# An adaptive-norm block with attention and routed experts: GpSimd's order bound by edges, experts' numbers read earlier, tile fills moved behind the first norm

## The chip, the cores and the metric

One Trainium2 chip, one of its cores. A core has TensorE (PE, with its weight loads PEld), VectorE (DVE), ScalarE (ACT), GpSimd (POOL) and SyncE (SP), each with an instruction stream of its own, and DMA queues that are issued from SP, ACT and POOL. The metric is the device time of one execution in microseconds (us), lower is better.

## The reference

A transformer block over x of 4 x 512 x 256, all in float32: a modulated layer norm, causal attention with 32 heads of 8 (8 key heads), a gated residual, a second modulated norm, then 16 routed experts (4 of them per token, chosen within 2 of 4 groups) plus a shared expert, and a second gated residual.

```python
mod = (_silu(L0_c) @ L0_wmod).reshape(L0_c.shape[0], 6, 1, -1)
sa, ca, ga, sb, cb, gb = (mod[:, 0], mod[:, 1], mod[:, 2], mod[:, 3], mod[:, 4], mod[:, 5])
ga = (2 * (ga >= 0) - 1) * jnp.maximum(jnp.abs(ga), 0.25)
gb = (2 * (gb >= 0) - 1) * jnp.maximum(jnp.abs(gb), 0.25)
h = _layernorm(x, axis=-1) * (1 + ca) + sa
x = x + ga * _L0_attn_ref(h, L0_attn_wq, L0_attn_wk, L0_attn_wv, L0_attn_wo)
h = _layernorm(x, axis=-1) * (1 + cb) + sb
x = x + gb * _L0_ffn_ref(h, ...)

# _L0_attn_ref: q, k, v projections, softmax(q k^T / sqrt(8), causal) v, projection wo
# _L0_ffn_ref:
cw = _combine_weights(xt, gate_w)          # softmax, 2 of 4 groups, top 4, normalized
out = jnp.zeros_like(xt)
for e in range(E):
    a = _swiglu(xt @ expert_up_w[e].T)
    out = out + cw[:, e:e + 1] * (a @ expert_down_w[e].T)
out = out + _swiglu(xt @ shared_up_w.T) @ shared_down_w.T
```

## The kernel before

**A plan makes the order.** The kernel does not write its instructions down in sequence. Each step is added to a `Plan` with its engine, an estimated cost, what it needs, a due time and the buffers that it takes and gives. `plan.go` takes, again and again, the step that can start first by these estimates (the earlier due time breaks a tie) and only then emits its instructions. The block runs under a manual schedule for PE, DVE, ACT and SP: on these four the emitted order is the order on the chip. POOL is not in that list; there a scheduler of the framework orders the instructions itself, whatever order the plan had for them. Each engine runs its stream in order; an instruction that waits holds all behind it.

**Start.** SP loads x for the first batch, then c, the modulation weights and the projections' weights (L178, L482 to L487). DVE fills three pairs of key and query tiles, `kx` with -1 and `qx` with 0 (L489, L490); POOL makes constants and fills two `vaug` tiles with 0 and, for the softmax denominators, a 1 beside each head's values (L492, L495). `norm1` of batch 0 follows: `stats` on DVE (L585, L586), `root` (L590), `power` on POOL (L594), `normalize` on DVE (L599), transposes on PE (L643), the modulation on ACT (L650), for which `modulate_first` (L519) and `modulated` (L528, L529) prepare the factors. `split` projects queries and keys (L695), cuts them into three bf16 parts (L705 to L718) and stores them to DRAM (L723); `project_v` and `place` (L750, L761) put the values into `vaug`. `load(s)` brings the parts of one pack of heads into `qx[s % 3]` and `kx[s % 3]` (L778 on SP, L783 on ACT for the first two packs, on SP later). After that SP issues the later loads (x of the other batches, gate, shared and output weights) and `blank_all`, which clears the two accumulators `acc_d` in DRAM.

**Attention** runs over 16 packs s, four for each batch. `row_max` multiplies queries by keys (L821), masks (L829) and takes row maxima on DVE (L842); `shift` turns the maxima into three rows of `qx` (L881, L891, L901). `pack` multiplies again with the maxima in place (L962), ACT takes the exponential (L974, tile `ex`, five buffers), POOL zeroes what lies above the diagonal (L980, 12 selects a pack), and `weigh` multiplies by `vaug` on PE (L932). After a batch's fourth pack, `after` projects by `wo` (L1081) and gates on DVE (L1091, tile `ao`), POOL adds to x (L1099), and `norm2` normalizes again: POOL's `power` (L594) and `modulate` (L1126, L1127, four times two instructions), the router's logits and choice on DVE, and then 16 indirect DMAs from POOL (L1297), each of which scatters 128 token rows from `row` (one buffer) to the lists of their experts in `rows_d`. Batches 0 to 2 do this while later packs run; batch 3 after attention.

**Experts.** `make_table` on DVE finds for each of 79 blocks of 128 rows its expert (`of_i`) and its first row (`row_i`). The shared expert's steps (L394 to L448) run on PE among and before the first blocks. A block j goes: `fetch` on SP (seven buffers of x), `turn` on PE (transposes, tile pt, L1454), `copy` on ACT (xt, L1458), `meta` on DVE (token and weight, L1463, L1466), `up` on PE (pu, L1474), `silu` on ACT (L1484), `product` on DVE (a_b, L1488), `turn_back` on PE (pb, L1493), `copy_back` on DVE (at_b, L1497), `down` on PE (py, L1502), `weigh` on ACT (y_b, L1512), and `put` on POOL: an indirect DMA that adds 128 rows into `acc_d[j % 2]` (L1515). `up` and `down` read the weights at an address that depends on the expert: `read` (L367) loads the block's number from SBUF into a register of PE's sequencer, at the beginning of `up`:

```python
def up():
    st["e"] = read(t["of_i"], j, PE, E - 1)
    st["pu"] = psu.tile([P, 2 * I], F32, name="pu")
```

In the order that the plan made, a steady period on PE is pu(42), py(41), pt(44), pb(42), then the load of number 43 and pu(43). At the end the two accumulators are read back, summed, gated and added to x (L1567 to L1578).

Of the kernel before, what the change touches and what calls it, by code (L numbers as in the profile page):

```python
# [151 lines left out]
def kernel(  # L152
# [122 lines left out]

    def hold(name, bufs=1):
        return rooms.setdefault(name, Room(bufs)).hold()
# [97 lines left out]
    def shared(b, due, up_bank, down_bank, first=None):  # L375
# [3 lines left out]
        def unit(n):  # L379
# [45 lines left out]
            for i in range(half // P):  # L425
# [20 lines left out]
                def put(i=i):  # L446
                    xs = x_sb[:, b * NT + n * half // P + i, :]
                    nc.gpsimd.tensor_tensor(xs, xs, st["o", i], ALU.add)  # L448
# [7 lines left out]
                plan.add("POOL", 0.75, put, [ga], due(), gives=[o_hold])  # L456
# [9 lines left out]
    def attention():  # L466
        with ExitStack() as ectx:
# [20 lines left out]
            for n, (q, k) in enumerate(zip(qx, kx)):  # L488
                nc.vector.memset(k, -1.0)  # L489
                nc.vector.memset(q, 0.0)  # L490
            for t in vaugs:
                nc.gpsimd.memset(t, 0.0)  # L492
                for g in range(NG):
                    one = VW * (g % SLOTS) + HD
                    nc.gpsimd.memset(t[:, :, g, one : one + 1], 1.0)  # L495
# [8 lines left out]
            plan.free.update(PE=6.0, ACT=4.0, DVE=5.0, POOL=8.0, SP=4.0)  # L504
# [71 lines left out]
            def layernorm(b, needs, due):  # L576
# [15 lines left out]
                def power():  # L592
                    st["rs"] = work.tile([P, NT], F32, name="rs")
                    nc.gpsimd.tensor_tensor(st["rs"], st["ve"], mhalf, ALU.pow)  # L594
# [20 lines left out]
                op = plan.add("POOL", 1.05, power, [op], due())  # L615
# [16 lines left out]
            def norm1(b, due):  # L632

                first = [later, weighed.get(NPK * (b - 1) - 1)] if b else []
                st, ops, h = layernorm(b, [first, [], [], []], due)
                ht_hold = hold("ht")
# [105 lines left out]
            def project_v(b, last, due, ht_hold):  # L742
# [24 lines left out]
                valued[b] = plan.add("ACT", 0.6, place, [op], due(), gives=[p_hold])  # L767
# [3 lines left out]
            def load(s):  # L771

                loaded[s] = []
                needs = [stored[True, s], stored[False, s], scored.get(s - 3)]
# [175 lines left out]
            def scores(s, j, c, r, n, exs, last, due):  # L950
# [27 lines left out]
                def select():  # L978

                    nc.gpsimd.affine_select(  # L980
                        out=st["ex"][:, :, 0:P],
                        in_=st["ex"][:, :, 0:P],
                        pattern=[[0, n], [1, P]],
                        base=0,
                        channel_multiplier=-1,
                        compare_op=ALU.is_ge,
                        fill=0.0,
                    )
# [6 lines left out]
                return pe, plan.add("POOL", 0.18 + 0.115 * n, select, [op], due), ex_hold  # L995
# [46 lines left out]
            def after(b, due):  # L1042
# [31 lines left out]
                for half in range(NT // 2):  # L1074
# [22 lines left out]
                    def put(half=half):  # L1097
                        xs = x_sb[:, b * NT + 2 * half : b * NT + 2 * half + 2, :]
                        nc.gpsimd.tensor_tensor(xs, xs, st["ao", half], ALU.add)  # L1099
# [9 lines left out]
                    adds.append(plan.add("POOL", 1.27, put, [ga], due(), gives=[ao_hold]))  # L1109
# [4 lines left out]
            def norm2(b, adds, due):  # L1114
# [5 lines left out]
                for i in range(NT):  # L1120

                    def modulate(i=i):
                        if i == 0:
                            st["row"] = work.tile([P, NT, XW], F32, name="row", bufs=1)
                        h = st["row"][:, i, 0:D]
                        nc.gpsimd.tensor_tensor(h, ln["xn"][:, i, :], m2_sb[:, b, 1, :], ALU.mult)  # L1126
                        nc.gpsimd.tensor_tensor(h, h, m2_sb[:, b, 0, :], ALU.add)  # L1127

                    rows.append(
                        plan.add(  # L1130
                            "POOL", 1.5, modulate, [ops[i], gates_made, *rows[-1:]], due(),
                            takes=[row_hold] if i == 0 else [],
                            gives=[ln_hold] if i == NT - 1 else [],
                        )
                    )
# [160 lines left out]
                def scatter(i, k):  # L1296
# [9 lines left out]
                    writes.append(dma.ins)  # L1306

# [19 lines left out]
                for i in range(NT):  # L1327
                    for k in range(TOPK):
                        final = i == NT - 1 and k == TOPK - 1
                        op = plan.add(  # L1330
                            "POOL", 1.3, lambda i=i, k=k: scatter(i, k), [op], due(),
                            lag=4.0 if final else 0.0 if b == B - 1 else 1.5, gives=[row_hold] if final else [],
                        )
# [24 lines left out]
            norm1(0, Pace(-8.0, -4.0, 40))  # L1358
            load(0)
# [24 lines left out]
    def ffn():  # L1384
# [48 lines left out]
        def block(j):  # L1433
# [17 lines left out]
            def turn():  # L1451
                st["pt"] = pst.tile([P, KC, P], F32, name="pt2")
                for k in range(KC):
                    nc.tensor.transpose(st["pt"][:, k, :], st["x"][:, ts(k, P)], ident)  # L1454

# [14 lines left out]
            def up():  # L1470
                st["e"] = read(t["of_i"], j, PE, E - 1)
# [52 lines left out]
            needs = [made, fetched[-1] if fetched else None]  # L1524
            if j == 0:
                needs += [*blanked, routed[B - 1]["rows"]]
            fe = plan.add("SP", 0.9, fetch, needs, due - 8, takes=[h["x"]])
            fetched.append(fe)
            op = plan.add("PE", 0.38, turn, [fe], due - 1.5, takes=[h["pt2"]])
# [5 lines left out]
                "PE", 1.45, up, [xt, weights], due, takes=[h["pu"]], gives=[h["xt"]]  # L1535
# [5 lines left out]
            op = plan.add("PE", 0.3, turn_back, [op], due + 0.6, takes=[h["pb"]], gives=[h["a_b"]])  # L1541
# [3 lines left out]
            op = plan.add("PE", 1.03, down, [op], due + 1.1, takes=[h["py"]], gives=[h["at_b"]])  # L1545
# [7 lines left out]
        fetched = []  # L1553
# [85 lines left out]
```

## Time and profile before

| | |
|---|---|
| median of three runs | 812.01 us (811.62 to 815.63) |
| the profiled execution | 819.83 us, its span 817.9 us |
| granted TensorE clock, mean over the span | 0.942 |
| start and first projections | 0 to 35 us |
| attention, 16 packs | 34 to 462 us |
| shared expert, routing of batch 3 | 462 to 560 us |
| expert blocks alone | 560 to 785 us |
| read-back and output | 785 to 818 us |
| PE busy, 150 to 200 / 200 to 250 / 250 to 300 us | 48.63 / 39.13 / 48.73 us |
| POOL: selects L980, 192 | 93.2 us busy, 491 ns each |
| POOL: scatters L1297, 64 | 63.9 us busy, 998 ns each |
| POOL: accumulating scatters L1515, 79 | 123.3 us busy, 1561 ns each |
| number loads on PE's sequencer, 79 | 295 / 507 / 585 ns (min / median / max) |

Times in a timeline are counted from the span's start. A line of the timeline has start, length, engine, line of the code, operation, output and input tiles, count, and in brackets the idle time of that engine just before, with what ended it. Matmuls are pipelined and their ends are modelled, so that PE's starts are safer to compare than its ends. Releasers are inferred from semaphores; where the engine named had long been done, it was another. The times below are worked out from the profiled execution.

### The profile page before, as it was taken

What the parts mean: (1) busy time and instruction counts of PE and PEld (TensorE: products, weight loads), DVE (VectorE), ACT (ScalarE), POOL (GpSimd) and SP (SyncE); (2) the same over time, 40 slices, a digit from 0 to 9 for tenths busy, and PEclk for the clock granted to TensorE, in tenths of its full rate; (3) what the DMA queues carried; (4) which work ended last, traced back from release to release, by engine and by line L of the source; (5) the groups of instructions that cost most, each with busy time, mean ns of one, the idle gap of its engine ahead of it and who ended that gap; (6) DMA issues with size and microseconds to landing.
All of it is one profiled execution on the core that took longest, in us unless ns stands there. A gap on an engine that the chain in (4) does not pass through costs nothing.

```text
span 817.9 us, 12877 instructions
## 1 busy us (share of the span) xinstructions
PE 686.4 (84%) x4205; PEld 417.4 (51%) x4236; DVE 454.4 (56%) x1286; ACT 309.9 (38%) x557; POOL 346.2 (42%) x449
## 2 busy tenths in 40 slices
PE   4568999999779998699968794999999999999930
PEld 3344455454434544245523483787666666666620
DVE  5395877878658887387854058343333333333318
ACT  1105655655345545264534510123333333333310
POOL 3001222344652355533555254514555555555533
PEclk9787999999999999899989997899999999999975
DMA  3484220202312023111111196604655655555465
GB/s 122 114 283 146 52 57 21 54 19 53 112 67 58 9 67 106 62 39 37 39 50 64 42 283 213 155 16 66 100 92 93 97 93 94 93 92 92 51 156 185
DMA packets 54969, 74.51 MB, mean 91 GB/s; under 512 B 8024, under 2 KB 48056, under 8 KB 53752
## 3 DMA queue, kind: packets, MB, share of 16 engines
q1 hardware_dynamic: 37992, 51.99, 22.8%
q0 software_dynamic: 14448, 19.31, 14.7%
q10 hardware_dynamic: 2464, 2.39, 0.9%
q8 instruction: 35, 0.57, 0.3%
q14 instruction: 30, 0.25, 0.1%
HBM read 41.11 MB, written 32.16 MB: 90 GB/s over the span
## 4 chain that ended last, share of the span: by engine, by line
PE 62%; DVE 19%; ACT 6%; issue 5%; POOL 4%; DMA 3%; another core or an unknown queue 1%; ACTq 0%; DVEq 0%; POOLq 0%
PE pu L1474 14%; PE py L1502 8%; PE pa L932 8%; PE pr L821 7%; DVE mx_s L842 6%; PE p L962 5%; PE pu L394 4%; ACT y_b L1512 4%; PE pr L829 3%; PE py L432 3%; PE p L543 2%; POOL rows_d L1297 2%; ACT ex L974 1%; PE p L695 1%; DMA s<-acc_d 1%
## 5 line engine op out<-in xcount | busy, mean ns | idle before, releaser
L842 DVE TENSOR_REDUCE mx_s<-pr 128x1 f32<-128x384 f32 (+3 forms) x352 | 213.2, 635 | 92.1 <-PE pr L829 67.4
L974 ACT ACTIVATE ex<-p 128x1024 f32<-128x1024 f32 (+1 forms) x192 | 163.5, 880 | 134.0 <-PE p L962 90.3
L980 POOL TENSOR_SCALAR_AFFINE_SELECT ex<-ex 128x256 f32<-128x256 f32 (+1 forms) x192 | 93.2, 491 | 206.9 <-ACT ex L974 205.1
L1515 POOL DMA_INDIRECT acc_d<-y_b,token x79 | 123.3, 1561 | 108.4 <-ACT xt L1458 97.7
L821 PE MATMUL pr<-kx,qx 125*128 125x384 bf16 (+3 forms) x512 | 127.2, 313 | 28.9 <-DVE mx_s L842 15.8
L1474 PE MATMUL pu<-up_sb,xt 128*128 x316 | 113.6, 482 | 12.7 <-ACT y_b L1512 11.4
L932 PE MATMUL pa<-ex,vaug 128*32 128x512 f32 (+3 forms) x1024 | 104.9, 452 | 20.0 <-POOL ex L980 10.5
L962 PE MATMUL p<-qx,kx 128*128 128x384 bf16 (+3 forms) x481 | 92.6, 300 | 6.0 <-DMA qx<-mrow 3.0
L1488 DVE TENSOR_TENSOR a_b<-sg_b,pu 128x176 f32<-128x176 f32 x79 | 26.7, 338 | 118.1 <-ACT sg_b L1484 118.1
L829 PE MATMUL pr<-seen,ident_h 128*128 128x128 bf16 (+2 forms) x352 | 89.5, 254 | 0.0
L821 PEld LDWEIGHTS <-qx 125*128 125x128 bf16 x512 | 47.4, 102 | 79.5 <-issue 51.8
L1502 PE MATMUL py<-down_sb,at_b 88*128 x316 | 81.4, 379 | 1.1 <-DVE at_b L1497 1.1
L1474 PEld LDWEIGHTS pu<-up_sb,xt 128*128 128x128 f32 x316 | 53.6, 189 | 47.7 <-ACT y_b L1512 26.6
L1297 POOL DMA_INDIRECT rows_d<-row,slot x64 | 63.9, 998 | 29.4 <-issue 16.2
L1502 PEld LDWEIGHTS py<-down_sb,at_b 88*128 88x128 f32 x316 | 59.7, 189 | 21.8 <-ACT y_b L1512 0.8
L1484 ACT ACTIVATE sg_b<-pu 128x176 f32<-128x176 f32 x79 | 25.1, 317 | 101.0 <-PE pu L1474 89.2
L962 PEld LDWEIGHTS <-kx 128*128 128x128 bf16 x512 | 41.2, 99 | 37.9 <-issue 23.1
L1512 ACT ACTIVATE y_b<-py,cw_b 128x256 f32<-128x256 f32 x79 | 37.4, 473 | 46.3 <-PE py L1502 46.3
L1497 DVE COPY at_b<-pb 88x256 f32<-88x256 f32 x79 | 33.2, 421 | 36.5 <-PE pb L1493 34.9
L932 PEld LDWEIGHTS pa<-ex,vaug 128*32 128x32 f32 x1024 | 22.3, 108 | 60.9 <-issue 34.0
L829 PEld LDWEIGHTS <-ident_h 128*128 128x128 bf16 x352 | 35.2, 100 | 31.0 <-issue 24.6
L394 PE MATMUL pu<-h2t,sup_sb 128*128 128x256 f32 (+1 forms) x192 | 47.8, 399 | 2.3 <-DVE a L414 1.7
(176 smaller groups left out, 760.1 us busy)
## 6 DMA issues: line engine op xcount, KB each, us to landing
x<-rows_d SPq DMA_DIRECT2D x79, 136.5 KB
qx<-qd SPq DMA_DIRECT2D x48, 192.0 KB
up_sb<-in_up_t SPq DMA_DIRECT2D x8, 704.0 KB
acc_d<-blank SPq DMA_DIRECT2D x2, 2176.0 KB
qd<-pt SPq DMA_DIRECT2D x16, 192.0 KB
down_sb<-in_down_t SPq DMA_DIRECT2D x8, 352.0 KB
rows_d<-blank SPq DMA_DIRECT2D x17, 136.5 KB
x_sb<-in_x SPq DMA_DIRECT2D x4, 512.0 KB
```

Source lines behind the costliest of these rows:

```text
L394: nc.tensor.matmul(st["p"][:rows, w, :], lhsT=sup_sb[:, k, c0 : c0 + rows], rhs=h2t[:, k, c1 : c1 + half], start=(k == 0), stop=(k == KC - 1),
L821: nc.tensor.matmul(pr[:, h, :], lhsT=qx[s % 3][:QKZ, REP * j + r + h, ts(i, P)], rhs=kx[s % 3][:QKZ, j, :w], start=True, stop=False, skip_ ...
L829: nc.tensor.matmul(pr[:, :, w - P :], lhsT=ident_h, rhs=seen.unsqueeze(1).to_broadcast([P, n, P]), start=False, stop=True, skip_group_chec ...
L842: nc.vector.tensor_reduce(mx[s][:, i, c0 : c0 + n], st["pr"], AX.X, ALU.max)
L932: nc.tensor.matmul(st["pa"][32 * r : 32 * r + 32, c * P :], lhsT=vaugs[b % 2][:, c, SLOTS * n + j, :], rhs=exs[r], start=(j == 0 and c == ...
L962: nc.tensor.matmul(pe[:, h, :], lhsT=kx[s % 3][:, j, ts(c, P)], rhs=qx[s % 3][:, REP * j + r + h, c * P :], start=True, stop=True,)
L974: nc.scalar.activation(ex, st["pe"], AF.Exp, scale=qk_scale)
L980: nc.gpsimd.affine_select(out=st["ex"][:, :, 0:P], in_=st["ex"][:, :, 0:P], pattern=[[0, n], [1, P]], base=0, channel_multiplier=-1, compa ...
L1297: dma = nc.gpsimd.indirect_dma_start(out=rows_d, out_offset=bass.IndirectOffsetOnAxis(ap=st["slot"][:, i, k : k + 1], axis=0), in_=st["row ...
L1474: nc.tensor.matmul(st["pu"], lhsT=st["xt"][:, k, :], rhs=up_sb[:, bass.ds(st["e"], 1), k, :].rearrange("p e f -> p (e f)"), start=(k == 0) ...
L1502: nc.tensor.matmul(st["py"], lhsT=st["at"][:, c, :], rhs=down_sb[:, bass.ds(st["e"], 1), c, :].rearrange("p e d -> p (e d)"), start=(c == ...
L1515: nc.gpsimd.indirect_dma_start(out=acc_d[j % 2], out_offset=bass.IndirectOffsetOnAxis(ap=st["token"][:, 0:1], axis=0), in_=st["y"], in_off ...
```

## The change

Three things. First, every POOL step of the plan is wrapped in `on_pool`, which adds an order-only dependency (no wait on the chip) from the instruction of POOL before it in the plan's order; scatters (`writes=True`) are ordered against what is not a scatter, but not among each other. Second, `read` moves from `up` to the end of `turn`, the planned costs of the block's PE steps change, and the planned chain from fetch to fetch is dropped. Third, the fills of `kx`, `qx` and `vaug` become steps of the plan: pair 0 and both `vaug` behind the last normalization of batch 0, pairs 1 and 2 behind the first query store; `load` and `place` now need them. The planned start times of the engines change a little.

```diff
+    stretches = [(False, []), (False, [])]
+
+    def on_pool(f, writes=False):
+        def run():
+            ins = [i.ins for i in f()]
+            if stretches[1][0] != writes:
+                stretches[:] = [stretches[1], (writes, [])]
+            (_, before), (_, same) = stretches
+            if not writes:
+                earlier = same[-1:] or before
+            else:
+                earlier = before[-1:]
+            nosync = mybir.DependencyInfo(
+                mybir.DependencyClass.NoSync, mybir.DependencyReason.DATA
+            )
+            for i in earlier:
+                tc.add_manual_dep(ins[0], i.name, nosync, reason="order on POOL")
+            same += ins
+
+        return run
...
-            for n, (q, k) in enumerate(zip(qx, kx)):
-                nc.vector.memset(k, -1.0)
-                nc.vector.memset(q, 0.0)
-            for t in vaugs:
-                nc.gpsimd.memset(t, 0.0)
+
+            def unused(n):
+                nc.vector.memset(kx[n], -1.0)
+                nc.vector.memset(qx[n], 0.0)
+
+            def denominators(t):
+                ins = [nc.gpsimd.memset(t, 0.0)]
                 for g in range(NG):
                     one = VW * (g % SLOTS) + HD
-                    nc.gpsimd.memset(t[:, :, g, one : one + 1], 1.0)
+                    ins.append(nc.gpsimd.memset(t[:, :, g, one : one + 1], 1.0))
+                return ins
+
+            filled, summed = [], []
+
+            def fill(after_it):
+
+                filled.append(plan.add("DVE", 2.7, lambda: unused(0), [after_it], -6.5))
+                for n, t in enumerate(vaugs):
+                    summed.append(
+                        plan.add(
+                            "POOL", 3.6, on_pool(lambda t=t: denominators(t)), [after_it], n - 6.5
+                        )
+                    )
...
-            plan.free.update(PE=6.0, ACT=4.0, DVE=5.0, POOL=8.0, SP=4.0)
+            plan.free.update(PE=6.5, ACT=5.0, DVE=5.0, POOL=6.0, SP=4.0)
...
-                op = plan.add("POOL", 1.05, power, [op], due())
+                op = plan.add("POOL", 1.05, on_pool(power), [op], due())
...
+                if b == 0:
+                    fill(ops[-1])
...
-                valued[b] = plan.add("ACT", 0.6, place, [op], due(), gives=[p_hold])
+                valued[b] = plan.add("ACT", 0.6, place, [op, summed[b % 2]], due(), gives=[p_hold])
...
-                needs = [stored[True, s], stored[False, s], scored.get(s - 3)]
+                needs = [stored[True, s], stored[False, s], scored.get(s - 3), filled[s % 3]]
...
-                return pe, plan.add("POOL", 0.18 + 0.115 * n, select, [op], due), ex_hold
+                return pe, plan.add("POOL", 0.18 + 0.115 * n, on_pool(select), [op], due), ex_hold
...
-                            "POOL", 1.3, lambda i=i, k=k: scatter(i, k), [op], due(),
+                            "POOL", 1.3, on_pool(lambda i=i, k=k: scatter(i, k), True), [op], due(),
...
             norm1(0, Pace(-8.0, -4.0, 40))
+            filled += [
+                plan.add("DVE", 2.7, lambda n=n: unused(n), [stored[False, 0]], -3.0)
+                for n in (1, 2)
+            ]
...
                 for k in range(KC):
                     nc.tensor.transpose(st["pt"][:, k, :], st["x"][:, ts(k, P)], ident)
+                st["e"] = read(t["of_i"], j, PE, E - 1)
...
             def up():
-                st["e"] = read(t["of_i"], j, PE, E - 1)
                 st["pu"] = psu.tile([P, 2 * I], F32, name="pu")
...
-            needs = [made, fetched[-1] if fetched else None]
-            if j == 0:
-                needs += [*blanked, routed[B - 1]["rows"]]
+            needs = [made, *blanked, routed[B - 1]["rows"]]
             fe = plan.add("SP", 0.9, fetch, needs, due - 8, takes=[h["x"]])
-            fetched.append(fe)
-            op = plan.add("PE", 0.38, turn, [fe], due - 1.5, takes=[h["pt2"]])
+            op = plan.add("PE", 0.25, turn, [fe], due - 1.5, takes=[h["pt2"]])
...
-                "PE", 1.45, up, [xt, weights], due, takes=[h["pu"]], gives=[h["xt"]]
+                "PE", 1.28, up, [xt, weights], due, takes=[h["pu"]], gives=[h["xt"]]
...
-            op = plan.add("PE", 0.3, turn_back, [op], due + 0.6, takes=[h["pb"]], gives=[h["a_b"]])
+            op = plan.add("PE", 0.25, turn_back, [op], due + 0.6, takes=[h["pb"]], gives=[h["a_b"]])
...
-            op = plan.add("PE", 1.03, down, [op], due + 1.1, takes=[h["py"]], gives=[h["at_b"]])
+            op = plan.add("PE", 0.87, down, [op], due + 1.1, takes=[h["py"]], gives=[h["at_b"]])
```

The steps `put` (twice, L448 and L1099), `modulate` (L1126) are wrapped in `on_pool` in the same way as `power`; the accumulating scatter (L1515) is not. The steps return their instructions, so that the edges can be set.

## The prediction, made before the changed kernel was run

> **What bounds the kernel now.** I read the page's shares and its chain of waits first, then busy time in 10 us stretches, then the timelines of the three places that the change touches.
>
> ```profile
> PE 686.4 (84%) x4205; PEld 417.4 (51%) x4236; DVE 454.4 (56%) x1286; ACT 309.9 (38%) x557; POOL 346.2 (42%) x449
> PE 62%; DVE 19%; ACT 6%; issue 5%; POOL 4%; DMA 3%; another core or an unknown queue 1%; ACTq 0%; DVEq 0%; POOLq 0%
> ```
>
> TensorE (PE) carries the chain, so the question is where it stands still. The next rows give, for each stretch, busy time (and count) of PE, PEld, DVE, ACT, POOL, then the granted clock, DMA share and GB/s.
>
> ```profile
> 200.00:210.00 10.00, 9.38 (x95) 5.76 (x95) 9.52 (x39) 6.25 (x11) 2.26 (x5) 1.00 0.18 44
> 210.00:220.00 10.00, 7.74 (x67) 3.35 (x64) 7.41 (x19) 4.38 (x6) 7.16 (x9) 1.00 0.45 135
> 220.00:230.00 10.00, 4.50 (x28) 1.95 (x28) 2.83 (x5) 2.32 (x3) 8.10 (x10) 1.00 0.31 107
> 230.00:240.00 10.00, 7.80 (x54) 3.24 (x59) 4.92 (x12) 3.43 (x5) 5.82 (x10) 0.83 0.16 58
> ```
>
> Elsewhere in attention (80 to 170) PE is busy 9.84 of 10 on average. From 210 to 240 it loses 10 us while POOL is full. POOL's timeline says with what:
>
> ```profile
> 219.64 0.96 POOL L1297 DMA_INDIRECT rows_d<-row,slot  x1 [0.30 <-issue]
> 220.91 0.96 POOL L1297 DMA_INDIRECT rows_d<-row,slot  x1 [0.30 <-issue]
> 221.88 0.41 POOL L980 TENSOR_SCALAR_AFFINE_SELECT ex<-ex 128x256 f32<-128x256 f32 x1
> 222.47 0.98 POOL L1297 DMA_INDIRECT rows_d<-row,slot  x1 [0.17 <-issue]
> ```
>
> A batch's 16 scatters of token rows run in bursts of up to four, 1.27 us each start to start, and the mask selects (L980), for which `weigh` on PE waits, stand behind them. 320 to 350 and 420 to 440 look the same: three batches scatter inside attention.
>
> In the expert blocks one period reads like this (DVE, PE, then the load of the expert's number on PE's sequencer: count, ns min/median/max, start):
>
> ```profile
> 614.99 0.34 DVE L1488 TENSOR_TENSOR a_b<-sg_b,pu 128x176 f32<-128x176 f32 x1 [1.60 <-ACT sg_b L1484]
> 615.31 0.38 PE L1454 MATMUL pt<-ident,x 128*128 128x128 f32 x2
> 615.53 0.38 PE L1493 MATMUL pb<-ident,a_b 128*88 128x128 f32 x2
> 616.08 1.45 PE L1474 MATMUL pu<-up_sb,xt 128*128 x4 [0.17 <-ACT y_b L1512]
> 617.37 1.03 PE L1502 MATMUL py<-down_sb,at_b 88*128 x4
> L367 PEldq TENSOR_LOAD <-of_i x1: 489/489/489, 615.4 to 615.4; - x1
> ```
>
> pb's work is 0.22 (so is pt's), yet pu starts 0.55 after pb. The load starts at 615.4, just after a_b ends (615.33): the sequencer stood at pb's wait for a_b, then loads for 0.49, then needs about 0.2 for address and first weights. It is the same in the eight other periods I looked at (612.4 after 612.35, 618.3 after 618.25, 641.6 after 641.55). The named ACT y_b had ended (615.98). So the period is a loop of latencies, pu to silu to product to load to pu. Where a_b comes early, the gap is gone:
>
> ```profile
> 556.99 0.34 DVE L1488 TENSOR_TENSOR a_b<-sg_b,pu 128x176 f32<-128x176 f32 x1 [1.12 <-ACT sg_b L1484]
> L367 PEldq TENSOR_LOAD <-of_i x1: 298/298/298, 557.4 to 557.4; - x1
> 559.20 0.38 PE L1493 MATMUL pb<-ident,a_b 128*88 128x128 f32 x2
> 559.41 0.76 PE L1474 MATMUL pu<-up_sb,xt 128*128 x2
> ```
>
> Here the load is issued 2 us ahead, with py, pt and pb still queued on PE, and pu follows pb after 0.21.
>
> At the start VectorE fills the q and k tiles before it looks at x:
>
> ```profile
> 5.12 0.21 ACT L509 ACTIVATE sct<-ct 128x8 f32<-128x8 f32 x1 [3.05 <-DMA ct<-in_c_t]
> 6.52 3.54 PE L519 MATMUL p<-sct,wmod_sb 128*128 128x4 f32 x16 [6.52 <-DMA wmod_sb<-in_wmod]
> 8.79 1.76 DVE L490 MEMSET qx<- 128x2048 uint32 x1 [0.38 <-issue]
> 10.47 0.37 DVE L585 BATCH_NORM_STATS2 bn<-x_sb 128x6 f32<-128x256 f32 x1
> ```
>
> **Part 1, fills behind the first norm.** x's load was issued before ct's on one queue, and ct had landed by 5.1; so the statistics can start at about 5.1 instead of 10.47. They, POOL's power and three normalizations take 4.8 by today's rows (10.47 to the end of the third at 15.3, less about 0.3 for mod_t in between): 9.6. In the changed order mod_t comes next and waits for PE L519, which ends at 10.06; the last normalization then ends near 10.8 against 15.36. Take **4.5**. Bounds: 5.5 if nothing waits for L519, 0 if what follows eats it. The moved fills cost 3.2 each (0.91 + 1.76 + two pauses). The first lies in DVE's idle stretch before L709 (15.7 to 21.1 today), the others in 25.1 to 29.5 and 31.8 to 35.4, before the first row maxima; there about 1.7 us of slack is left, and without that cover each costs up to 3.2. POOL's fills (3 us) end near 12 and are needed at 26 (L761). The store of the third projection falls behind the later loads on SP; its reader, load(2), stands behind both already. Blanks and first mrow come after it in the queue and move along. On ACT's queue the second copy of that projection (L714) falls behind three more key loads (0.5 each), which brings the first keys forward a little and the copy, needed by the same late store, back: nothing.
>
> **Part 2, POOL bound to the plan.** No instruction is added; edges of order only. In the changed program's POOL order a batch's 16 scatters stand nearly all singly between one to three selects, over 25 selects in batch 0 (2.1 packs of 12), in place of bursts over 7 selects. PE's order in attention is the same. What can come back: PE idle above its usual 0.16 per 10 us, 9.5 (210 to 240) + 9.3 (320 to 350) + 6.7 (420 to 440) = 25.5; and the clock, 0.83, 0.83 and 0.63/0.85 in and after the stalls, worth 1.3 + 2.4 + 2.9 (PE's busy time times the missing share) = 6.6. Together 32. What spreading costs: a select then waits up to 1.27 behind one scatter, which the five ex buffers should absorb. The nearest rows are 180 to 190 and 390 to 400, POOL busy 8.32 and 9.53 with pieces of 0.4 to 1.3: PE still 9.18 and 9.77, losing 0.07 to 0.66 beyond its usual. Over some 15 stretches 1 to 10; take 5. **27**, bounds 10 (more than twice the dearest row) and 32. The last four scatters of batch 2 fall behind the last select, where POOL is idle today (462 to 470): nothing.
>
> Here a rule stands against the change. The Trainium skill (SBUF — State Buffer, Who interferes with whom) has GpSimd fully blocked, descriptor writing too, while VectorE runs a two-port instruction, and never by a reduce. The trace shows one scatter of 1.84 among VectorE's table work (502.69) against 0.96 to 1.06; at that price 48 scatters would need 42 us more of POOL, spread over the 150 us in which it is half idle. By the rule the gain would lean to the lower bound; VectorE's largest group there is reduces (213 us), so I keep 27.
>
> **Part 3, numbers read earlier.** The load moves from `up` into `turn`, and with the new costs each block's turn-back (pb) stands one block later: PE's order is pu(42), py(40), pb(41), pt(44), load(44), pu(43). Nothing in it waits for the product of the pu just before. at_b(40) is ready about 0.4 after pu(42) starts, and then the sequencer runs to the load with about 2 us of queued work, as at 557.4. So the period falls to PE's own work: 1.19 (pu to the next row where there was no gap: 549.68 to 550.87) + 0.87 + 0.22 + 0.22 = 2.50; I take 2.55. Today: pu(3) at 559.41 to pu(75) at 771.66, 212.25 / 72 = 2.95. 72 x 0.40 = **28.5**. Other engines per period: ACT 1.15, DVE 1.16, POOL 1.56 + 0.28. Fetches run six blocks ahead; their planned chain goes, SP's order of them does not. Next in line is the accumulating scatter, which waits for the one two before it on the same acc_d: start to completion was 3.87 at the end (783.94 to 787.81), so a period of (3.87 + 0.28) / 2 = 2.1; from above, today's fastest periods of 2.77 show no such wait, so at worst 2.77 and a gain of 13. Bounds 0 and 32. The first three blocks among the shared expert and the drain keep their order: nothing.
>
> The Trainium skill (Advanced Engine Details and Errata, Sequencer Loop) says engine instructions are queued and wait there while control instructions run. By that the load would not stand behind pb's wait, and moving it would give 0; the trace disagrees, with each load starting within 0.1 of a_b's end.
>
> **Sum.** 4.5 + 27 + 28.5 = 60. Profiled execution: 819.8 (span 817.9 + 1.9) - 60 = 760. It was 7.8 above the median of the runs, 812.0; so **752**.
>
> **Rivals.** (a) The gap is not the load's but the sequencer's before a register-addressed matmul, or the load stops everything wherever it stands: 812 - 31.5 = 780. Against it: 557.4. (b) Spreading only moves PE's waits: selects are late singly, attention gives 10 or less: about 769. For it: POOL's work is the same; against: 390 to 400. (c) Slower: POOL's order is now fixed, and the 24 power, residual and modulate instructions of three batches stand at planned places; where VectorE is late they hold the selects behind them. POOL's waits for `ao` (L1099) came to 21.4 in 8, mean 2.7; 24 x 2.7 = 64 gives 816. It decides from 2.5 each. Against it: today's order has the same neighbours within a few selects, without such holes in PE. (d) The edges do nothing and the reads nothing: 808 to 812; against it, the changed orders.
>
> **How the numbers follow.** Forecast 0.70 (742 to 768 by itself), (a) 0.07, (b) 0.15, (c) 0.05, (d) 0.03. The range 738 to 782 holds the forecast, (a) and (b). Half a per cent (4 us) is what a measurement of this kernel can tell from no change. Faster 0.93, same 0.02 (part of d), slower 0.05.
>
> **What would show it.** First statistics at 5 us; PE above 9 of 10 wherever scatters run, each scatter alone, clock 1.00; pu to pu 2.5 to 2.6, pu following pt without a gap, loads starting over 1 us before their pu. Wrong if the load still ends just before pu, if a DMA on acc_d is named before POOL L1515, or if POOL waits for VectorE with selects behind.

## The result, and the profile after

The changed kernel took **745.24 us** (median of 4 runs, 744.14 to 746.31) beside 813.82 us for the kernel before in the same comparison (4 runs, 811.62 to 817.42). The ratio is **0.915**, 95% interval [0.911, 0.919]: faster by 68.6 us. A second comparison later gave 0.914 [0.910, 0.917]. The profiled execution has a span of 744.4 us against 817.9.

The page of the changed kernel, first the busy times and then the shares of the chain that ended last:

```profile
PE 651.1 (87%) x4205; PEld 411.5 (55%) x4236; DVE 455.6 (61%) x1286; ACT 317.4 (43%) x557; POOL 346.2 (47%) x449
PE 66%; DVE 17%; DMA 6%; POOL 3%; issue 3%; ACT 2%; ACTq 0%; another core or an unknown queue 0%; SPq 0%; DVEq 0%; POOLq 0%
```

The work is the same (PE's 4205 instructions, POOL's 346.2 us), yet PE is "busy" for 35 us less. The records of the same instructions are shorter: `pa` of attention takes 96.8 us in all where it took 104.9, `pu` of the expert blocks 106.6 where it took 113.6. So time came back both from gaps and from within the busy share.

The 10 us stretches of attention that lost most before, and three at its end (busy time and count of PE, PEld, DVE, ACT, POOL, then granted clock, DMA share, GB/s):

```profile
210.00:220.00 10.00, 9.47 (x81) 4.60 (x81) 8.02 (x15) 5.39 (x7) 7.22 (x12) 1.00 0.44 130
220.00:230.00 10.00, 9.75 (x94) 4.62 (x95) 7.94 (x18) 6.43 (x8) 6.83 (x11) 1.00 0.26 78
230.00:240.00 10.00, 9.75 (x83) 5.03 (x80) 8.26 (x16) 6.40 (x8) 7.82 (x12) 1.00 0.42 120
...
400.00:410.00 10.00, 5.86 (x50) 2.52 (x44) 2.58 (x8) 4.91 (x8) 5.92 (x9) 0.92 0.14 44
410.00:420.00 10.00, 9.35 (x65) 3.12 (x65) 0.00 (x0) 6.55 (x8) 6.45 (x12) 0.74 0.12 44
420.00:430.00 10.00, 7.56 (x47) 5.25 (x48) 0.78 (x2) 2.73 (x5) 5.12 (x7) 0.83 0.40 124
```

From 210 to 240 PE is busy 28.97 of 30 us, against 20.04 before, at a clock of 1.00 throughout, while POOL is as busy as it was. Over the whole kernel PE's idle time before `pa` that is put down to POOL's `ex` fell from 10.5 us to 1.0. The last three rows are the end of attention, where VectorE has no row maxima left to make (0.00 busy from 410 to 420) and PE waits for the last pack's chain; that stand-still was there before (440 to 470, 7.4 us idle, now 7.2) and has stayed. Its clock has not: it was 1.00 in those rows before and is 0.74 to 0.92 now.

POOL's timeline in the first of the three batches:

```profile
221.84 0.98 POOL L1342 DMA_INDIRECT rows_d<-row,slot  x1 [0.17 <-issue]
223.56 0.40 POOL L1020 TENSOR_SCALAR_AFFINE_SELECT ex<-ex 128x256 f32<-128x256 f32 x1 [0.74 <-ACT ex L1013]
224.25 0.41 POOL L1020 TENSOR_SCALAR_AFFINE_SELECT ex<-ex 128x256 f32<-128x256 f32 x1 [0.29 <-ACT ex L1013]
224.81 0.98 POOL L1342 DMA_INDIRECT rows_d<-row,slot  x1 [0.16 <-issue]
225.81 0.42 POOL L1020 TENSOR_SCALAR_AFFINE_SELECT ex<-ex 128x256 f32<-128x256 f32 x1
```

Each scatter here stands alone (in all three batches two pairs are left, and the last four of the third stand behind the last select), and two of the three selects wait for ScalarE's `ex`, not for POOL. The third follows a scatter at once, so it can have stood behind it for at most 0.98. POOL is ahead of its suppliers again.

One period of the expert blocks, with the load of the expert's number below it:

```profile
601.80 0.38 PE L1504 MATMUL pt<-ident,x 128*128 128x128 f32 x2
602.01 0.42 DVE L1547 COPY at_b<-pb 88x256 f32<-88x256 f32 x1 [0.40 <-PE pb L1543]
602.02 1.35 PE L1524 MATMUL pu<-up_sb,xt 128*128 x4
603.21 1.03 PE L1552 MATMUL py<-down_sb,at_b 88*128 x4
604.07 0.38 PE L1543 MATMUL pb<-ident,a_b 128*88 128x128 f32 x2
604.30 0.38 PE L1504 MATMUL pt<-ident,x 128*128 128x128 f32 x2
604.51 1.35 PE L1524 MATMUL pu<-up_sb,xt 128*128 x4
L389 PEldq TENSOR_LOAD <-of_i x1: 297/297/297, 602.6 to 602.6; - x1
```

pu to pu is 604.51 - 602.02 = 2.49, and pu starts 0.21 after pt, about as pt follows pb (0.23). at_b is ready at 602.43, 0.41 after pu's start; with it the last wait ahead of the load ends, the sequencer passes py, pb and pt and loads at 602.6, while PE still works on pu, and no matmul stands still for it. The load is also shorter: 0.30 at the median of all 79, against 0.51 before.

The start:

```profile
5.01 0.43 DVE L622 BATCH_NORM_STATS2 bn<-x_sb 128x6 f32<-128x256 f32 x1 [5.01 <-DMA x_sb<-in_x]
8.01 3.55 PE L556 MATMUL p<-sct,wmod_sb 128*128 128x4 f32 x16 [8.01 <-DMA wmod_sb<-in_wmod]
11.88 0.41 DVE L636 TENSOR_SCALAR xn<-x_sb,mv,rs 128x256 f32<-128x256 f32 x1
```

The statistics start with x at 5.01; the last normalization ends at 12.29 (15.36 before), later than the 10.8 forecast because `wmod` landed 1.5 later in this execution.

### The profile page after: what moved, and what is told of

Same layout as the page of the kernel before. It is cut to its first block, busy times and chain, and to the rows that moved or that the text cites. A ratio compares the mean times of both kernels' runs of the same rounds, so it can differ in the third digit from the quotient of the medians.

```text
span 744.4 us, 12881 instructions
## 1 busy us (share of the span) xinstructions
PE 651.1 (87%) x4205; PEld 411.5 (55%) x4236; DVE 455.6 (61%) x1286; ACT 317.4 (43%) x557; POOL 346.2 (47%) x449
## 4 chain that ended last, share of the span: by engine, by line
PE 66%; DVE 17%; DMA 6%; POOL 3%; issue 3%; ACT 2%; ACTq 0%; another core or an unknown queue 0%; SPq 0%; DVEq 0%; POOLq 0%
PE pu L1524 13%; PE py L1552 9%; PE pa L971 8%; PE pr L860 8%; PE p L1001 6%; DVE mx_s L881 6%; PE pu L416 5%; PE py L454 3%; PE pr L868 2%; PE pb L1543 2%; PE pt L1504 2%; DMA s<-acc_d 2%; PE p L580 1%; ACT ex L1013 1%; DMA kx<-kd 1%
## 5 line engine op out<-in xcount | busy, mean ns | idle before, releaser
L860 PE MATMUL pr<-kx,qx 125*128 125x384 bf16 (+3 forms) x512 | 125.2, 309 | 20.9 <-DVE mx_s L881 10.0
L1524 PE MATMUL pu<-up_sb,xt 128*128 x316 | 106.6, 460 | 0.0
L971 PE MATMUL pa<-ex,vaug 128*32 128x512 f32 (+3 forms) x1024 | 96.8, 450 | 2.5 <-POOL ex L1020 1.0
L416 PEld LDWEIGHTS pu<-h2t,sup_sb 128*128 128x128 f32 (+1 forms) x192 | 36.6, 193 | 9.8 <-DVE a L436 2.0
```

Source lines behind the costliest of these rows:

```text
L416: nc.tensor.matmul(st["p"][:rows, w, :], lhsT=sup_sb[:, k, c0 : c0 + rows], rhs=h2t[:, k, c1 : c1 + half], start=(k == 0), stop=(k == KC - 1),
L860: nc.tensor.matmul(pr[:, h, :], lhsT=qx[s % 3][:QKZ, REP * j + r + h, ts(i, P)], rhs=kx[s % 3][:QKZ, j, :w], start=True, stop=False, skip_ ...
L971: nc.tensor.matmul(st["pa"][32 * r : 32 * r + 32, c * P :], lhsT=vaugs[b % 2][:, c, SLOTS * n + j, :], rhs=exs[r], start=(j == 0 and c == ...
L1524: nc.tensor.matmul(st["pu"], lhsT=st["xt"][:, k, :], rhs=up_sb[:, bass.ds(st["e"], 1), k, :].rearrange("p e f -> p (e f)"), start=(k == 0) ...
```

## The experiments

In these comparisons the kernel before took about 821 to 823 us, so ratios to it are compared and not microseconds of different comparisons. "us" below is (1 - ratio) x 812, the median that the prediction started from.

### The three parts, each alone

The first is the kernel before with `on_pool` around POOL's operations and nothing else; the orders of PE, VectorE, ScalarE and SP are unchanged.

```diff
-  op = plan.add("POOL", 1.05, power, [op], due())
+  op = plan.add("POOL", 1.05, on_pool(power), [op], due())
...
-  "POOL", 1.3, lambda i=i, k=k: scatter(i, k), [op], due(),
+  "POOL", 1.3, on_pool(lambda i=i, k=k: scatter(i, k), True), [op], due(),
```

> The kernel before with the POOL edges alone (no moved fills, reads as before). Orders on PE, VectorE, ScalarE and SP are those of before, only POOL's order differs. Theory (bursts of scatters held the selects, spreading them gives PE's stalls and the lost clock back): the time falls by 27 to 38 us, to about 776 to 787; PE is busy over 9 of 10 from 210 to 350, no granted clock below 1.00 there. Rival (spreading only moves PE's waits): 10 us or less, 803 or more, with new idle time before pa or p spread over more stretches. Second rival (part of the 38 us between the first select and the shared expert comes from the earlier start or the fills): 15 to 25 us here.

Measured: 0.953 [0.949, 0.957], that is **38 us** [35, 42]. The theory's upper end holds; the rival of 10 us or less falls, and so does the one of 15 to 25. From 210 to 350 PE is busy at least 9.2 of every 10 us, at a clock of 1.00, as expected. Two of its stretches, the same columns:

```profile
220.00:230.00 10.00, 9.68 (x86) 4.64 (x83) 8.32 (x18) 6.28 (x9) 6.65 (x12) 1.00 0.17 58
230.00:240.00 10.00, 9.59 (x85) 4.78 (x83) 7.10 (x13) 5.70 (x8) 6.87 (x11) 1.00 0.47 132
```

Since PE's order is the same in both, the starts of the same selects can be set side by side (us from the start of the 67th select to that of the 85th, and so on, in the two profiled executions):

```text
selects          67-85   115-133   163-192   all others
kernel before     41.7     45.4      52.4      249.6
edges alone       30.3     30.6      42.8      248.9
difference        11.4     14.8       9.6        0.7
```

All but 0.7 of the time comes back at the three bursts, and between them nothing is lost. At the bursts a little may be: PE is still idle for 1.47 from 210 to 240 and 0.86 from 320 to 350, in place of its usual 0.48, so spreading costs some 1.0 and 0.4 us there (the third batch's scatters fall into the end of attention, where PE waits anyway).

The fills, moved as in the change, POOL's order left to itself:

```diff
+  filled.append(plan.add("DVE", 2.7, lambda: unused(0), [after_it], -6.5))
...
-  needs = [stored[True, s], stored[False, s], scored.get(s - 3)]
+  needs = [stored[True, s], stored[False, s], scored.get(s - 3), filled[s % 3]]
```

> The kernel before with the fills moved behind the first norm alone. Theory as predicted: 4.5 us, about 808.5. By the changed kernel's profile, where the first select came 2.0 us earlier and the last normalization 3.1: about 2 us, 811, within what a measurement can tell from nothing. Rival (the fills stand in front of row maxima and cost as much as they gave): 0 or a loss of up to 5.

Measured: 0.995 [0.993, 0.997], **4.0 us** [2.2, 5.8]: as predicted, not 0. Only repeated executions show it: in single profiles the 7th select began at 84.1 (kernel before), at 86.0 (edges alone) and at 82.3 (reads alone), though none of the three moves the fills, so the start varies by 4 us between executions.

The reads with their costs and needs:

```diff
   def turn():
+      st["e"] = read(t["of_i"], j, PE, E - 1)
   def up():
-      st["e"] = read(t["of_i"], j, PE, E - 1)
...
-  op = plan.add("PE", 1.03, down, [op], due + 1.1, ...)
+  op = plan.add("PE", 0.87, down, [op], due + 1.1, ...)
```

> The kernel before with the experts' numbers read in the turn and the new planned costs, so that PE's order is pu(42), py(40), pb(41), pt(44), load(44), pu(43); POOL's order as before. Theory: pu to pu falls from 2.95 to 2.49 to 2.55, 72 periods, 28 to 33 us; time about 780 to 785. Rival (the accumulating scatter or VectorE is next in line at 2.77): 13 us, 799.

Measured: 0.965 [0.962, 0.968], **28.5 us**; silu to silu over 72 blocks 2.511 (before 2.949). The rival at 2.77 falls.

The product of the three ratios, 0.953 x 0.995 x 0.965 = 0.915, is that of the whole change: the parts neither help nor hinder each other.

### What about the reads is worth the time

The change does two things: the load stands in the turn, and by the new costs the turn-back (pb) stands one block later. First only the place, with the old costs:

```diff
   def turn():
+      st["e"] = read(t["of_i"], j, PE, E - 1)
   def up():
-      st["e"] = read(t["of_i"], j, PE, E - 1)
```

> The kernel before with only the place of the load changed (in the turn, old planned costs), so PE's order is pu(42), py(41), pt(44), load(44), pb(42), pu(43): the load no longer stands behind pb's wait for a_b, but pb(42) still waits for the product of the pu just before. Theory (a loop of latencies, of which the load is 0.34 of the 0.55 from pb to pu): the period falls from 2.95 to about 2.6, 72 x 0.34 = 24 us, time about 788, and pu to pu stays above PE's own work of 2.49. Rival A (the load alone was the cost): the full 33 us, 780. Rival B (what counts is only that the turn-back stands one block later): 5 us or less.

Measured: 0.964 [0.961, 0.967], 29 us, and a period of 2.526 over 72 blocks, 2.49 in the steady part. Its timeline:

```profile
612.04 0.34 DVE L1488 TENSOR_TENSOR a_b<-sg_b,pu 128x176 f32<-128x176 f32 x1 [1.11 <-ACT sg_b L1484]
612.35 0.39 PE L1454 MATMUL pt<-ident,x 128*128 128x128 f32 x2
612.58 0.38 PE L1493 MATMUL pb<-ident,a_b 128*88 128x128 f32 x2
612.79 1.35 PE L1474 MATMUL pu<-up_sb,xt 128*128 x4
613.98 1.03 PE L1502 MATMUL py<-down_sb,at_b 88*128 x4
614.53 0.34 DVE L1488 TENSOR_TENSOR a_b<-sg_b,pu 128x176 f32<-128x176 f32 x1 [1.11 <-ACT sg_b L1484]
614.84 0.38 PE L1454 MATMUL pt<-ident,x 128*128 128x128 f32 x2
615.07 0.38 PE L1493 MATMUL pb<-ident,a_b 128*88 128x128 f32 x2
615.28 1.05 PE L1474 MATMUL pu<-up_sb,xt 128*128 x3
L367 PEldq TENSOR_LOAD <-of_i x1: 415/415/415, 613.6 to 613.6; - x1
```

pb still starts 0.2 after the end of the a_b of the pu just before (612.38, 612.58), yet pu follows at 0.21 and the period is PE's own. Without the load, the loop of latencies (1.74 from pu to a_b, 0.34, 0.20, 0.21) comes to 2.49, just what PE's work comes to; no run shows that this is more than chance. My 2.6 was too high: the 29 us [27, 32] lie between its 24 and rival A's 33 and exclude both, while the steady period of 2.49 and the fact that nothing is left for the other half to add are rival A's.

Then the opposite, the new costs with the load ahead of its own pu:

```diff
-  op = plan.add("PE", 0.38, turn, [fe], due - 1.5, takes=[h["pt2"]])
+  op = plan.add("PE", 0.25, turn, [fe], due - 1.5, takes=[h["pt2"]])
...
-  op = plan.add("PE", 0.3, turn_back, [op], due + 0.6, ...)
+  op = plan.add("PE", 0.25, turn_back, [op], due + 0.6, ...)
```

> The kernel before with the new planned costs and without the planned chain of fetches, but the load where it was, just ahead of its own pu: PE's order is pu(42), py(40), pb(41), pt(44), load(43), pu(43), the same as with both but for the block whose number is loaded. Theory (the load cost time only because the sequencer reached it late, behind a wait that had just ended; with the turn-back one block later nothing before the load is waited for): the period is 2.49 to 2.55 as with both, 28 to 33 us, time 780 to 785, though no number is read two blocks ahead. Rival (the number has to be read ahead, or load, address and first weights show before each pu): period 2.8 or more, a gain of 11 us or less, 801 or more.

Measured: 0.958 [0.952, 0.965], 34 us [29, 39]; period 2.511, as with both. One load in its steady part starts at 611.7, its pu at 613.56:

```profile
611.07 1.35 PE L1474 MATMUL pu<-up_sb,xt 128*128 x4
612.25 1.03 PE L1502 MATMUL py<-down_sb,at_b 88*128 x4
613.12 0.38 PE L1493 MATMUL pb<-ident,a_b 128*88 128x128 f32 x2
613.34 0.38 PE L1454 MATMUL pt<-ident,x 128*128 128x128 f32 x2
613.56 1.35 PE L1474 MATMUL pu<-up_sb,xt 128*128 x4
L367 PEldq TENSOR_LOAD <-of_i x1: 308/308/308, 611.7 to 611.7; - x1
```

So no number has to be read two blocks ahead. It is enough that every wait between the last pu and the load ends while PE is still at work on that pu; the place does that, the order does that, and the second of them adds nothing.

### How much a select can wait

To bring bursts back into the changed kernel, scatters were held back in the plan and issued together, four or eight at a time:

```diff
+  def grouped(i, k, size=4):
+      n = i * TOPK + k
+      if b < B - 1 and n % size < size - 1:
+          return lambda: kept.append((i, k))
+      def several():
+          kept.append((i, k))
+          ins = [dma for at in kept for dma in scatter(*at)]
+          kept.clear()
+          return ins
+      return on_pool(several, True)
```

> The changed kernel with the scatters of three batches issued on POOL in groups of four (three are held back to the place of the fourth); all other orders the same. A group takes POOL 4 x 1.27 = 5.1 us. Theory (the length of a burst is what holds the selects): with about 2 us of cover by the ex buffers each of 12 groups costs 1 to 3 us, so 12 to 36 us more than the changed kernel, 757 to 781, with PE idle at the groups. Rival (POOL's share is what counts, or the buffers cover 5 us): within 4 us of 745.

> As the last, in groups of eight: 10.2 us each, 6 groups. Theory: 6 x (10.2 - 2) = 49 us more than the changed kernel, about 794; if the cover is nearer 5 us, 6 x 5 = 30, about 775, while groups of four cost nearly nothing. Rival (POOL's share): within 4 us of 745.

Measured: 0.949 [0.945, 0.952] and 0.953 [0.949, 0.958], some 28 and 31 us above the changed kernel. **These two don't measure what they were made for.** `on_pool` binds only the first instruction of what it is given; the other scatters of a group ran ahead, and POOL's order came out nearly that of the kernel before in both (in batch 0 two, one, four, three scatters with one select between). That the 28 falls into the range expected for fours is therefore luck. What they do show: with the selects, the residual adds and the fills all bound, loose scatters alone lose about three quarters or more of what the edges gave.

With every scatter bound, pairs and fours stand where they were meant to:

```diff
+  def grouped(i, k, size=4):
+      def run():
+          kept.append((i, k))
+          if b == B - 1 or len(kept) == size:
+              for at in kept:
+                  on_pool(lambda: scatter(*at), True)()
+              kept.clear()
+      return run
```

> The changed kernel itself, to stand beside the three that follow on the same chip. Its ratio to the kernel before was 0.915 [0.911, 0.919]; the three parts alone gave 0.953, 0.995 and 0.965, whose product is 0.915. Expected: 0.911 to 0.919 again.

> The changed kernel with three batches' scatters in pairs, each scatter of a pair bound to its place (in the earlier groups only the first was bound and the others ran ahead, back into bursts over seven or eight selects). 2 x 1.27 = 2.5 us of POOL per pair, with two to four selects between pairs. Theory of the backlog (PE loses only what POOL falls behind by more than the ex buffers cover; 16 scatters over 8 selects are 20.3 + 8 x 0.5 us of POOL against 8 x 1.85 of PE's pace, 9.5 behind): nothing, within 4 us of the changed kernel. Rival (each time a select waits longer than about 1.3, PE waits too): 24 pairs x 1.2 = up to 29 us more.

> The same in fours, each bound: 5.1 us of POOL per group, five or six selects between groups. Theory of the backlog: POOL is 5.1 behind and catches up before the next group; with a cover of 4 to 5 us at most 1 us is lost at each of 12 groups, 0 to 12 us more than the changed kernel. Rival (the length of a burst counts by itself): 12 x 3 = 36 us more, as much as the whole gain of the edges.

Measured on one chip: singly 0.914 [0.910, 0.917], in pairs 0.915 [0.912, 0.919], in fours 0.940 [0.935, 0.944]. Pairs cost nothing that the runs can tell (751.73 against 750.23); fours cost 20.5 us (770.78 - 750.23), 1.7 for each of 12. The backlog's 0 to 12 is passed and the rival's 36 not reached; a cover shorter than I had put it would do that. PE and POOL at one group of four:

```profile
219.91 0.84 PE L971 MATMUL pa<-ex,vaug 128*32 128x384 f32 x4
220.74 0.96 POOL L1342 DMA_INDIRECT rows_d<-row,slot  x1 [0.30 <-issue]
222.01 0.96 POOL L1342 DMA_INDIRECT rows_d<-row,slot  x1 [0.30 <-issue]
222.99 1.59 POOL L1020 TENSOR_SCALAR_AFFINE_SELECT ex<-ex 128x256 f32<-128x256 f32 x3
223.46 0.84 PE L971 MATMUL pa<-ex,vaug 128*32 128x384 f32 x4 [2.71 <-POOL ex L1020]
```

Three selects had come due behind the group, PE waited 2.71 for the first of them, and that POOL kept it from running is named in the row. By pairs (2.5 us of POOL, no loss) and fours (5.1, 1.7 lost on average) the `ex` buffers cover more than 2.5 and less than 5.1 us; 5.1 - 1.7 = 3.4 is an estimate that leaves aside what the lower clock behind a group (0.83 and 0.90 from 220 to 240) adds to the loss.

### A stand-still that is left

Behind attention PE waits for VectorE, which makes the table of blocks in one piece:

```profile
463.45 1.47 DVE L345 TENSOR_TENSOR gone<-last,number 128x1264 f32<-128x1264 f32 x1
463.91 1.84 POOL L1342 DMA_INDIRECT rows_d<-row,slot  x1 [0.30 <-issue]
464.96 1.47 DVE L352 TENSOR_REDUCE of<-gone 128x79 f32<-128x1264 f32 x1
466.06 0.96 POOL L1342 DMA_INDIRECT rows_d<-row,slot  x1 [0.30 <-issue]
466.46 1.47 DVE L356 TENSOR_TENSOR is_of<-expert,of 128x1264 f32<-128x1264 f32 x1
467.32 1.45 POOL L1342 DMA_INDIRECT rows_d<-row,slot  x1 [0.30 <-issue]
467.97 1.48 DVE L365 TENSOR_TENSOR gone<-is_of,first 128x1264 f32<-128x1264 f32 x1
469.07 1.20 POOL L1342 DMA_INDIRECT rows_d<-row,slot  x1 [0.30 <-issue]
...
473.24 1.22 PE L454 MATMUL py<-sdown_sb,a 96*128 96x256 f32 x2 [8.98 <-DVE a L436]
```

`py` waited 8.98 for a product that stood behind the table. Two versions put the table later, the second also in single steps:

```diff
-  made = make_table(fp, counted, 60.0)
+  made = make_table(fp, counted, 250.0)
...
-  (counts, 0.9), (starts, 0.9), (of, 2.8), (is_of, 1.4), (base, 2.8), (rows, 1.0)
+  (counts, 0.9), (starts, 0.9), (of, 1.4), (of_sum, 1.4), (is_of, 1.4), (base, 1.4), (base_sum, 1.7), (rows, 1.0)
```

> The changed kernel with a later due time for the table of blocks on VectorE (250 in place of 60), so that the shared expert's products go ahead of its ten 0.4 to 1.5 us steps. In the changed kernel PE stands still from 464.3 to 473.2 behind them, at a granted clock of 0.67 after it. Theory: 6 to 10 us less than the changed kernel, 735 to 739. Rival (the table comes later, so do the fetches and the first blocks, and PE runs out of shared work): 0, or up to 5 us more.

> The changed kernel with the table's due time at 250 and its two longest steps (two and three VectorE instructions) cut into single ones, so that the shared expert's products go between them. The due time alone gave 0.906 [0.900, 0.911] against the kernel before, on another chip run than the changed kernel. Theory: PE's stand-still behind the table (9 us at 464.3 to 473.2) shrinks to about 3, 6 to 10 us less than the changed kernel, ratio to the kernel before 0.903 to 0.909. Rival (PE's wait moves to the end of the shared expert, or to the first blocks): no more than 2 us apart from the changed kernel.

Measured: 0.906 [0.900, 0.911] and 0.907 [0.903, 0.911], the second beside 0.914 [0.910, 0.917] for the changed kernel on the same chip: 744.43 against 750.23, **5.8 us**. All six runs with the single steps (741.09 to 747.65) lie below all five of the changed kernel (749.92 to 753.46), so the gain is real though under 1%, and the rival's 2 us or less falls; the 6 to 10 expected are just missed. For the due time alone the changed kernel was not run beside it. In single profiles PE's idle time from 450 to 490 was 10.2 us with the single steps and 15.4 in the changed kernel beside it: a third went, and what is left lies mostly at 450 to 460 and 480 to 490, 4.0 each.

## Why the prediction was right, and where it was off

The forecast was 752 by a sum of 60; the change gave 0.085 x 812 = 69. The mechanism was that of the forecast in all three parts, and one size was off.

- **Part 1, 4.5 forecast, 4.0 measured** [2.2, 5.8]. The statistics did start at 5. In the profile of the fills alone the last normalization ended at 11.20 and the first row maxima began at 30.88, 4.5 before the 35.38 of the kernel before: the fills stayed hidden.
- **Part 2, 27 forecast, 38 measured** [35, 42], above the upper bound of 32. This is the mis-sized term. Its step "a select then waits up to 1.27 behind one scatter, which the five ex buffers should absorb ... take 5" took off 5 for spreading; the idle time above shows 1.0 and 0.4 for two of the three batches, and pairs of scatters show that even 2.5 us are absorbed. The dearer of the two rows it was taken from (180 to 190, PE 9.18) holds no scatter but POOL's `modulate`, and the changed kernel still shows 9.17 there: that idle time is not what spreading brings. The rest is the bound itself: 32.1 by idle time and clock, where the selects show 11.4 + 14.8 + 9.6 = 35.8. The 3.7 that it left out lie inside PE's busy rows or just outside the stretches that were counted; no run here separates the two.
- **Part 3, 28.5 forecast, 28.5 measured**, period 2.55 forecast, 2.49 in the steady part and 2.51 over 72. That the two sums are equal is partly luck: the period fell by 2.949 - 2.511 = 0.44, which over 72 blocks is 31.5, and some 3 of that did not reach the whole time. What was wrong is the reading of which half of the edit does it: I had it that the new order lets the load run early, and counted on both halves. Either alone takes the load off the loop. The bounds named for the next engine didn't act: POOL's put was held by a DMA on acc_d once, for 2.2 us, and VectorE's `token`, which needs a buffer that a put frees, 18 times for 20.6 us, with PE at 10.00 of 10 from 490 to 700.
- **The step from the profiled execution to the median** (819.8, 7.8 above 812.0) did no harm. The kernel before took 812 to 814 in the first comparisons and 821 to 823 in the later ones, and the changed kernel 745 and 750; the ratio was 0.915 and 0.914.
- **The rivals.** (a), a gap that isn't the load's: its 780 would need pu to start late after pt; it starts at once. (b), spreading moves PE's waits: 10 or less forecast, 38 measured. (c), the fixed order holds selects: POOL's waits for `ao` (L1140) came to 18.2 in 8, mean 2.3 where 2.5 was to decide. Two of the eight, 8.4 together, lie behind the last select; the six inside attention (0.57 to 3.27) are as long as in the kernel before, and PE was busy all through them.
- **Signs not met**: the clock is not 1.00 wherever scatters run. From 400 to 430 it is 0.74 to 0.92, where PE waits for the last pack's chain; the waits there that are put down to POOL's `ex` come to 2.1 us in 6, the longest 0.5.

The prediction read one lengthened scatter (1.84) in VectorE's table work; the kernel before has two more behind it there, 1.44 and 1.21, and so has the changed kernel. In attention, where VectorE's largest group is reduces, 48 scatters took 0.98 at the median and 1.23 at most, and POOL's busy time stayed at 346.2 us. So the rule of the Trainium skill (SBUF — State Buffer, Who interferes with whom) by which the gain would lean to its lower bound did not decide here. Beside the table the scatter that began under a TENSOR_REDUCE took 0.96, which agrees with the page's "never" for reduces. The three that began under a TENSOR_TENSOR took 1.84, 1.45 and 1.20, the longer the more of that instruction was still to come (1.01, 0.62 and 0.38), as if each waited for its end. The page counts a TENSOR_TENSOR with two SBUF inputs as holding GpSimd's reads and infers that descriptors can still be written; whether these scatters were held at the read of `slot` or at their descriptors, no run here shows.

The rule of the Trainium skill (Advanced Engine Details and Errata, Sequencer Loop), as the prediction read it, has a load not stand behind an instruction that waits: the runs disagree. In the kernel before 74 of the 79 loads started less than 0.1 after an a_b had ended; in the changed kernel the median load started 0.19 after an at_b had ended and 1.9 before the next pu. Moving the load alone brought 29 us, and moving the waiting pb alone 34; in each the load ran during the pu before, with py and pt (and in the second pb) still ahead of it in the queue, so work whose waits have ended is passed, and only a wait still open holds the sequencer.

## What to carry to other kernels

Count how long a consumer on a shared engine can be kept waiting before the bound engine notices (here more than the 2.5 us of a pair of scatters and less than the 5.1 of a four), and keep foreign work below that in one go; its sum, the same 346.2 us of POOL in both kernels, then cost nothing that was seen. Where a sequencer must load a value, look at what stands just ahead of the load in the queue: a wait that ends at the last moment makes the load a part of the loop, and moving either of the two is enough. An order that is to hold must bind every instruction: binding the first of a group left the others free to run back into bursts.

## What the runs showed of the hardware

- The load of a number on PE's sequencer took 0.30 at the median where it ran ahead and 0.51 where it stood right behind the wait; the period before was longer by 0.46, of which pu's later start is 0.34 and pu's longer row (1.45 against 1.35) 0.10.
- The same orders start attention up to 4 us earlier or later from one execution to the next (7th select at 82.3 to 86.0), as much as the whole first part; one profile can't size an edit there.
- A stand-still of PE can come with a lower clock, and then costs beyond its own length: around the table the clock was 0.67 for 20 us, and in the stretch with the group of four (220 to 230) 0.83, where the singly placed scatters had 1.00. Not every one does: from 440 to 470 of the kernel before PE was idle for 7.4 us in all, at 1.00.
